# A state space stage whose output stands channels by tokens: paired TensorE products, and decays along tokens read back through DRAM

## The chip, the cores and the metric

The kernel runs on one core of one Trainium2 chip. The metric is the device time of one execution in microseconds (us). The core has a matrix engine (TensorE, PE in the profile; its weight loads are shown apart as PEld), a vector engine (VectorE, DVE), a scalar engine (ScalarE, ACT), GpSimd (POOL) and a sync engine (SyncE, SP), which here issues nearly all direct DMAs. Each engine runs its own instructions strictly in the order in which they stand in its queue; they wait for one another through semaphores. TensorE writes to PSUM, of which the kernel uses eight banks: four as single tiles named `bank`, four as two double tiles named `banks`.

## The reference, cut to what matters

The model is a convolution and attention layer on an image (2 x 256 channels x 48 x 48), a state space (Mamba 2) layer on the 2 x 2304 tokens that it gives, and a routed layer of eight experts. Only the middle one is touched. For a token with normed input `xn` it computes

```
z, x, B, C, dt = split(W_in xn)            # 512, 512, 64, 64, 8 (heads of 64 channels)
x, B, C        = silu(conv over 4 tokens)
dt             = softplus(dt + dt_bias);  a = dt * -exp(A_log)          # per head
state[head]    = exp(a) * state[head] + dt * outer(x[head], B)          # 64 x 64 per head
y[head]        = state[head] C + D[head] * x[head]
out            = W_out( rmsnorm(y * silu(z)) ) + residual
```

The recurrence is computed in chunks of 128 tokens: within a chunk by a masked product of decays and B C, between chunks by a carried state. The square mean of the RMS norm runs over all 512 channels of a token, so that its factor is one number per token and can be applied behind `W_out`.

## The kernel before

**Tiling.** The 4608 tokens are 36 chunks of 128 tokens; three chunks are a block of 384 (`NJ`, `TB`), so there are 12 blocks. `mamba` (L541) is a loop over steps, one chunk a step. In each step it issues the stages of a hand-written pipeline, the oldest chunk first: `out_stage` of the chunk four steps back, `turn_stage` of three back, `y_stage` of two back, `state_stage` and `decay_stage` of the last one and `token_stage` of this one. Every third step also issues the block's front stages: `norms`, `project_0`, `project_1`, `gates_0`, `gates_1` and `sums`. After every six chunks `gate` picks the experts of their tokens (a generator, spread over the stages of the following steps) and scatters the rows to the experts' table `xs`, two indirect DMAs per chunk, issued by GpSimd (L912). The final order of each engine's queue is fixed when the program is built: the instructions of neighbouring stages are mixed there.

**What a step does before the change.** y has tokens on partitions.

- `gates` (L654) multiplies normed tokens (as the stationary operand) with two slices of 264 columns of `W_in`: 256 of z, and 8 of dt or of the router. z is passed through Silu (L665); dt gets its bias (L669); the router's part is made into `gp` (L670). `sums` (L687) makes three short products of the log decays `a`: sums from the chunk's start, sums to its end, and totals; L697 and L699 take their exponentials, `ex` and `et`.
- `project_1` ends with Silu on x (`xc`, L635) and on B and C (`bc`, L636), and moves C to partitions 0 to 63 by a DMA (`ct`, L638).
- `token_stage` (L722): GpSimd spreads `a` over a 128 x 1024 mask, `al` (L730). TensorE transposes B (L734) and x (four times 128 x 128, L737) so that tokens are on partitions; ScalarE copies them out (`btt` L739, `xt` L741). VectorE makes `xd` = x dt (L743), GpSimd `xw` = xd times the decay to the chunk's end (L745), and `y` = x D (L747).
- `decay_stage` (L749): two products of 512 columns sum `al` (L755), ScalarE takes the exponential (`mt`, L764); the product of B and C (L760), masked (`gm`, L762), is multiplied in (L765).
- `state_stage` (L767): one product of 512 columns gives what the chunk adds to the state, on 64 partitions (L773); another of 512 columns with contraction 64 gives what the old state gives to y (L776). VectorE scales the old state (L781), adds (L782), and multiplies the other product by the decay from the chunk's start (`yi`, L784), which with tokens on partitions is one number per partition and head; GpSimd adds it to y (L785).
- `y_stage` (L787): eight products, one per head, with the 128 x 128 `mt` stationary and 64 columns of `xd` moving (L794); VectorE adds y (L795), GpSimd multiplies by z (L796), ScalarE squares and sums along the row (L799), and `rsqrt` (L164: one VectorE and one GpSimd instruction, L169 and L170) gives `rg`, one number per token.
- `turn_stage` (L803) transposes y in four pieces (`transposes`, L518: products at L525, a ScalarE copy at L527). `out_stage` (L811) multiplies with `W_out` (L821, 264 columns, four pieces), adds the residual (L825), and stores the rows to `acc` by a DMA on SP's queue (L832).

The convolution layer ahead of this stage is used in the prediction for comparison: its `score` (L408) multiplies two attention heads on the two halves of the array's rows, one after the other, and `mix` (L469) gives two heads to the two halves of its columns.

Of the kernel before, what the change touches and what calls it, by code (L numbers as in the profile page):

```python
# [55 lines left out]
ZH = DI // 2  # L56

ZG = ZH + SH
XBC = 2 * ZG
# [20 lines left out]
for _name, _k in (  # L80
    ("bq", NH), ("bk", NH), ("bv", NH), ("bp", 1), ("w1", NH * 9), ("w2", NH * 9), ("norm_w", NH),
    ("gnorm_w", DI // P), ("conv_w", NM * 4), ("conv_b", NM),
):
    _VEC[_name] = (_n, _n + _k)
    _n += _k
# [4 lines left out]
for _name, _k in (  # L90
    ("dt_bias", SH), ("A_log", SH), ("Dp", SH), ("bg", E), ("rate1", 1), ("rate2", 1),
):
    _ROW[_name] = (_n, _n + _k)
    _n += _k
# [32 lines left out]
class Kernel:  # L127
# [352 lines left out]
    def mamba_weights(self):  # L480
# [4 lines left out]
        wout = wts.tile([P, DI // P, C + E], F32, name="wout")  # L485
# [7 lines left out]
    def scale_weights(self):  # L493
# [3 lines left out]
        wg = [l1["win"][:, k, ZG + ZH : XBC] for k in range(NH)]  # L497
# [4 lines left out]
        for k in range(NH):  # L502
            for w in (l1["win"][:, k, : ZG + ZH], l1["win"][:, k, XBC:]):
                nc.gpsimd.tensor_scalar(w, w, v["norm_w"][:, k : k + 1], None, ALU.mult)
        turned = self.att.tile([P, NH, P], F32, tag="turned", name="turned", bufs=1)
        for m in range(DI // P):
# [34 lines left out]
    def mamba(self, ctx):  # L541
# [5 lines left out]
        front = (self.norms, self.project_0, self.project_1, self.gates_0, self.gates_1, self.sums)  # L547
        stages = ((self.out_stage, 4), (self.turn_stage, 3), (self.y_stage, 2), (self.state_stage, 1),
# [4 lines left out]
        for step in range(-NJ * 2, nchunk + 4):  # L553
            for p in reversed(range(len(front))):
                k, r = divmod(step + len(front) - 1 - p, NJ)
# [10 lines left out]
            done = step - 3  # L566
# [63 lines left out]
    def project_1(self, k):  # L630
# [3 lines left out]
        xc, bc = block["xc"], block["bc"]  # L634
        nc.scalar.activation(xc, xc, AF.Silu)  # L635
        nc.scalar.activation(bc, bc, AF.Silu)  # L636
        ct = block["ct"] = self.m.tile([DS, TB], F32, tag="ct", name="ct", bufs=3)
        nc.sync.dma_start(ct, bc[DS:P, :])  # L638
# [15 lines left out]
    def gates(self, block, j):  # L654

        nc = self.nc
        xn, win = block["xn"], self.l1["win"]
        cols = slice(3 + j * P, 3 + (j + 1) * P)
        ps = self.banks()
        for h in range(2):  # L660
            self.project(
                ps[:, h, :ZG], lambda k: xn[:, k, cols], lambda k: win[:, k, h * ZG : (h + 1) * ZG]
            )
        z = block["z", j] = self.m.tile([P, DI], F32, tag="z", name="z", bufs=7)
        nc.scalar.activation(z.rearrange("p (h q) -> p h q", h=2), ps[:, :, :ZH], AF.Silu)  # L665
        if j == 0:
            block["dt"] = self.small.tile([P, NJ, SH], F32, tag="dt", name="dt")
            block["gp"] = self.small.tile([P, NJ, E], F32, tag="gp", name="gp")
        nc.vector.tensor_tensor(block["dt"][:, j, :], ps[:, 0, ZH:ZG], self.r["dt_bias"], ALU.add)  # L669
        nc.vector.scalar_tensor_tensor(  # L670
            block["gp"][:, j, :], ps[:, 1, ZH:ZG], block["kap"][:, j : j + 1], block["msw"][:, j, :],
            ALU.mult, ALU.add,
        )

    def gates_0(self, k):
        for j in range(2):
            self.gates(self.blocks[k], j)

    def gates_1(self, k):
        nc, block = self.nc, self.blocks[k]  # L680
        self.gates(block, 2)
        dt = block["dt"]
        self.softplus(dt)
        a = block["a"] = self.small.tile([P, NJ, SH], F32, tag="a", name="a")
        nc.vector.tensor_tensor(a, dt, bcast(self.l1["na"], 1, [P, NJ, SH]), ALU.mult)

    def sums(self, k):  # L687

        nc, small, block = self.nc, self.small, self.blocks[k]
        n = NJ * SH  # L690
        a = block["a"].rearrange("p j s -> p (j s)")
        ps = self.bank()
        nc.tensor.matmul(ps[:, 0:n], lhsT=self.c["le"], rhs=a, start=True, stop=True)
# [499 lines left out]
```

## Time and profile before

| what | value |
|---|---|
| time, median of 3 runs | 1740.0 us (1737.6 to 1740.46) |
| the profiled execution | 1738.11 us, its span 1736.2 us |
| granted TensorE clock, mean | 0.933 of full |
| state space stage, about | 400 to 1065 us of the span |
| a step of it | first `al` products at 441.7 us, last chunk's at 1002.7 |
| instructions | 20936 |

One execution is recorded by the hardware profiler. The page first gives each engine's busy time and share of the span; then the span in 40 equal slices of 43.4 us, each digit the busy share in tenths, and in the row PEclk the clock that the chip granted to TensorE. Further views give groups of instructions (line, engine, operation, output and inputs, shapes, count, busy time and mean ns of one), the waits (who waited for whom: total us, times, longest us), the timeline (start us, length us, engine, line, operation) and the busy time in chosen stretches (for each engine busy us and instruction count). The start of an instruction in TensorE's timeline is sharp; its length reaches into the next one's, since products are pipelined. In float32 each product is recorded twice, and so is its weight load; a transpose is recorded once. "Idle before" is time in which the engine had nothing to run.

### The profile page before, as it was taken

Reading aid. Unit: us, or ns where it says so; the run is one execution under the profiler, and the core shown is the slowest. Engines: PE = TensorE matmul, PEld = TensorE weight load, DVE = VectorE, ACT = ScalarE, POOL = GpSimd, SP = SyncE. Lnnn points to the kernel's source line nnn. Section 1 sums busy time; section 2 is a strip of 40 time slices with the busy share of each in tenths; the row PEclk is TensorE's granted clock in tenths of the full one; section 3 lists DMA queues with packets and bytes.
Section 4 is the critical chain, followed back from the end, with each engine's and each line's share of the span. In section 5 each row is a group of like instructions: output and inputs, shape, how many; then the busy total and the mean of one; then the engine's idle time right before and its main releaser. Section 6 shows DMA issues by size and latency. Waiting matters only on the chain.

```text
span 1736.2 us, 20936 instructions
## 1 busy us (share of the span) xinstructions
PE 1532.9 (88%) x7366; PEld 1134.7 (65%) x7366; DVE 924.3 (53%) x2337; ACT 721.2 (42%) x1564; POOL 562.2 (32%) x505
## 2 busy tenths in 40 slices
PE   2999999987899879798897962999999999999994
PEld 1556565654566556464555542888888888888883
DVE  5867669996787878677786754111111111111111
ACT  0565667885655445453553410222222222222221
POOL 5020000001456565556656763122222222222220
PEclk9898999998998898898898975999999999999997
DMA  6222231111000010101001012666666666666646
GB/s 226 82 72 91 94 112 38 49 37 54 3 10 11 25 34 12 41 13 33 24 12 46 13 47 81 211 194 194 198 192 196 199 200 196 199 198 200 195 137 224
DMA packets 78658, 182.18 MB, mean 105 GB/s; under 512 B 7677, under 2 KB 69526, under 8 KB 72214
## 3 DMA queue, kind: packets, MB, share of 16 engines
q1 hardware_dynamic: 61894, 159.00, 26.3%
q0 software_dynamic: 15840, 21.05, 6.6%
q8 instruction: 59, 0.97, 0.2%
q10 hardware_dynamic: 820, 0.79, 0.1%
q14 instruction: 45, 0.37, 0.1%
HBM read 138.98 MB, written 47.95 MB: 108 GB/s over the span
## 4 chain that ended last, share of the span: by engine, by line
PE 66%; DVE 13%; POOL 8%; ACT 5%; DMA 3%; issue 2%; SPq 1%; DVEq 0%; POOLq 0%; ACTq 0%
PE bank L1023 17%; PE po L1037 17%; PE bank L539 4%; POOL xs L912 3%; PE banks L539 3%; PE bank L469 3%; PE bank L351 2%; PE bank L794 2%; PE bank L374 2%; PE bank L821 2%; PE bank L525 2%; DVE x L312 2%; PE bank L332 2%; PE banks L450 2%; PE banks L408 1%
## 5 line engine op out<-in xcount | busy, mean ns | idle before, releaser
L1027 ACT ACTIVATE hid<-bank,wt 128x256 f32<-128x256 f32 x344 | 163.0, 474 | 442.8 <-PE bank L1023 442.8
L1023 PE MATMUL bank<-ext,wt 128*128 128x256 f32 x1376 | 306.8, 381 | 1.0 <-DVE ext L527 0.8
L1037 PE MATMUL po<-wt,hid 128*128 128x256 f32 x1376 | 304.3, 379 | 0.0
L1043 POOL DMA_INDIRECT acc<-ey,ex x86 | 134.3, 1562 | 494.6 <-DVE ey L1041 334.9
L1023 PEld LDWEIGHTS bank<-ext,wt 128*128 128x128 f32 x1376 | 263.1, 191 | 38.0 <-DVE ext L527 1.2
L1037 PEld LDWEIGHTS po<-wt,hid 128*128 128x128 f32 x1376 | 258.2, 190 | 33.4
L527 DVE COPY ext<-bank 128x512 f32<-128x512 f32 x43 | 29.7, 692 | 281.9 <-PE bank L525 281.9
L1040 DVE TENSOR_TENSOR ey<-po,wt 128x256 f32<-128x256 f32 x86 | 36.5, 424 | 172.0 <-PE po L1037 171.9
L312 DVE SCALAR_TENSOR_TENSOR x<-hid,w2r,x 128x1128 f32<-128x1128 f32 (+3 forms) x72 | 99.2, 1379 | 0.6
L861 POOL TENSOR_SCALAR u<-cst 128x1 int32<-128x1 f32 x36 | 8.6, 246 | 279.0 <-PE bank L469 277.1
L539 PE MATMUL bank<-xn,win 128*128 128x387 f32 x240 | 94.1, 536 | 3.3 <-ACT xn L527 2.9
L426 ACT ACTIVATE prob<-prob,top 128x308 f32<-128x308 f32 x144 | 78.3, 548 | 34.3 <-DVE top L414 34.3
L652 DVE SCALAR_TENSOR_TENSOR xc<-bank,vec,xc 128x384 f32<-128x384 f32 x144 | 81.7, 611 | 20.0 <-ACT xc L648 19.2
L539 PE MATMUL banks<-win,xn 128*128 128x264 f32 x288 | 90.7, 451 | 0.0
L312 DVE SCALAR_TENSOR_TENSOR hid<-xp,vec,hid 128x1128 f32<-128x1128 f32 (+3 forms) x64 | 88.3, 1387 | 0.0
L912 POOL DMA_INDIRECT xs<-u,rows x72 | 75.7, 1052 | 35.3 <-issue 19.1
L755 PE MATMUL banks<-al,cst 128*128 128x512 f32 x144 | 78.2, 643 | 5.2 <-ACT mt L764 4.6
L730 POOL TENSOR_TENSOR al<-cst,a 128x1024 f32<-128x1024 f32 x36 | 68.6, 1913 | 43.7 <-DVE taken L902 14.5
L796 POOL TENSOR_TENSOR y<-y,z 128x512 f32<-128x512 f32 x36 | 47.1, 1307 | 106.7 <-DVE y L795 49.6
L469 PE MATMUL bank<-pt,val 110*64 110x128 f32 (+1 forms) x864 | 76.5, 282 | 4.4 <-ACT pt L453 4.3
L469 PEld LDWEIGHTS bank<-pt,val 110*64 110x64 f32 (+1 forms) x864 | 61.8, 138 | 26.8 <-issue 15.0
L794 PEld LDWEIGHTS bank<-xd,mt 128*128 128x128 f32 x576 | 71.3, 200 | 8.6 <-PE bank L525 3.5
(228 smaller groups left out, 2641.3 us busy)
## 6 DMA issues: line engine op xcount, KB each, us to landing
wt<-in_We SPq DMA_DIRECT2D x43, 2184.0 KB
ex<-xs SPq DMA_DIRECT2D x43, 265.0 KB
val<-vtab SPq DMA_DIRECT2D x72, 110.0 KB
vtab<-vraster SPq DMA_DIRECT2D x18, 396.0 KB
vraster<-vout SPq DMA_DIRECT2D x22, 256.0 KB
x<-in_x SPq DMA_DIRECT2D x4, 1152.0 KB
acc<-x SPq DMA_DIRECT2D x36, 128.0 KB
t<-acc SPq DMA_DIRECT2D x12, 384.0 KB
```

The source lines that it names most:

```text
L312: nc.vector.scalar_tensor_tensor(dst, src, w[:, k : k + 1], dst, ALU.mult, ALU.add)
L426: nc.scalar.activation(prob[:, a, :], prob[:, a, :], AF.Exp, bias=top[:, a : a + 1], scale=-1.0, accum_out=den[:, a : a + 1],)
L469: nc.tensor.matmul(po[j * HD : (j + 1) * HD, :P], lhsT=val[:nk, i, a * HD : (a + 1) * HD], rhs=pt[:nk, j, i, :], start=i == 0, stop=i == l ...
L539: self.nc.tensor.matmul(ps, lhsT=lhs(k), rhs=rhs(k), start=k == 0, stop=k == NH - 1)
L652: nc.vector.scalar_tensor_tensor(out, ps[:, i : i + TB], wc[:, i : i + 1], out, ALU.mult, ALU.add)
L755: nc.tensor.matmul(pd[:, k, :], lhsT=self.c["gt"], rhs=al[:, 4 * k : 4 * k + 4, :].rearrange("p s t -> p (s t)"), start=True, stop=True,)
L794: nc.tensor.matmul(py[:, cols], lhsT=mt[:, s, :], rhs=xd[:, cols], start=True, stop=True)
L912: put = nc.gpsimd.indirect_dma_start(self.xs, bass.IndirectOffsetOnAxis(ap=rows[:, i, k : k + 1], axis=0), u2[:, i, :], None)
L1023: nc.tensor.matmul(ps[:, :TR], lhsT=w1[:, k, c * P : (c + 1) * P], rhs=xt[:, k, :], start=k == 0, stop=k == NH - 1,)
L1027: nc.scalar.activation(hid[:, c, :], ps[:, :TR], AF.Gelu, bias=b1[:, c : c + 1])
L1037: nc.tensor.matmul(po, lhsT=hid[:, c, j * P : (j + 1) * P], rhs=w2[:, c, :], start=c == 0, stop=c == NHC - 1)
L1043: nc.gpsimd.indirect_dma_start(self.acc, bass.IndirectOffsetOnAxis(ap=token, axis=0), y[:, j, :], None, compute_op=ALU.add)
```

## The change

y now stands with channels on partitions (four pieces of 128 channels) and tokens along the row, from the start to `W_out`.

- z is made with the weights stationary, 384 tokens moving, four pieces of 128 channels per block (in `sums`); dt and the router's part come from six products of 16 columns per block (`gates`, one stage instead of two), and their VectorE work is done once per block.
- `y_stage` has `xd` (64 columns per head) stationary and `mt` (128 columns) moving, two heads to the two halves of the partitions.
- The state stands as 128 x 256: four heads on partitions 0 to 63, four on 64 to 127. What the chunk adds is two products of 256 columns; what the old state gives is four of 128 columns, with B and C taken from `ct` and from the upper half of `bc`.
- The decay from the chunk's start must now run along tokens. `sums` makes it for 8 heads x 384 tokens, stores it to DRAM (`decays`), and `token_stage` loads it back spread over partitions, `rd`, by two DMAs per chunk; neither chunk that begins an image needs it.
- x D is done by ScalarE, four instructions of 128 x 128; `xt` goes. ScalarE squares y, VectorE adds the four pieces up (`sm`), and a product with ones (`square_stage`, three steps back) sums over channels. `turn_stage` is gone; `out_stage` stands three steps back, behind `state_stage`.
- Silu on x, B and C and the DMA of `ct` move from `project_1` to the end of `sums`; `sums` comes one step earlier than it did.

```diff
-        front = (self.norms, self.project_0, self.project_1, self.gates_0, self.gates_1, self.sums)
-        stages = ((self.out_stage, 4), (self.turn_stage, 3), (self.y_stage, 2), (self.state_stage, 1),
+        front = (self.norms, self.project_0, self.project_1, self.gates, self.sums)
+        stages = ((self.square_stage, 3), (self.y_stage, 2), (self.state_stage, 1), (self.out_stage, 3),
                   (self.decay_stage, 1), (self.token_stage, 0))
...
-                k, r = divmod(step + len(front) - 1 - p, NJ)
+                k, r = divmod(step + len(front) - p, NJ)
...
     def gates(self, k):
+        ps = self.bank()
+        for j in range(NJ):
+            cols = slice(3 + j * P, 3 + (j + 1) * P)
             self.project(
+                ps[:, j * 2 * SH : (j + 1) * 2 * SH], lambda k: xn[:, k, cols], lambda k: win[:, k, DI:XBC]
+            )
...
     def sums(self, k):
+        for j in range(NJ):
+            nc.tensor.matmul(
+                ps[:SH, j * P : (j + 1) * P], lhsT=a[:, j, :], rhs=self.c["le"], start=True, stop=True
+            )
+        from_start = small.tile([SH, TB], F32, tag="from", name="from_start", bufs=2)
+        nc.scalar.activation(from_start, ps[:SH, :TB], AF.Exp)
+        nc.sync.dma_start(self.decays[k], from_start)
+        z = block["z"] = self.m.tile([P, NZ, TB], F32, tag="z", name="z")
+        for i in range(2):
+            ps = self.banks()
+            for m in range(2):
+                cols = slice((2 * i + m) * P, (2 * i + m + 1) * P)
+                self.project(ps[:, m, :TB], lambda k: win[:, k, cols], lambda k: xn[:, k, 3:])
+            nc.scalar.activation(z[:, 2 * i : 2 * i + 2, :], ps[:, :, :TB], AF.Silu)
+        nc.scalar.activation(bc, bc, AF.Silu)
+        nc.scalar.activation(xc, xc, AF.Silu)
+        nc.sync.dma_start(ct, bc[DS:P, :])
...
     def token_stage(self, c):
-        nc.scalar.copy(xt, px)
-        nc.gpsimd.tensor_tensor(hp(y), hp(xt), bcast(self.r["Dp"], 2, wide), ALU.mult)
+        for m in range(NZ):
+            nc.scalar.mul(y[:, m, :], block["xc"][:, m, cols], self.v["Dp"][:, m : m + 1])
+        if c % (NBLK * NJ):
+            rd = ch["rd"] = self.m.tile([P, NZ, P], F32, tag="rd", name="rd")
+            by_head = self.decays[c // NJ].rearrange("(m i) t -> i m t", i=2)
+            for i in range(2):
+                nc.sync.dma_start(
+                    rd[i * HD : (i + 1) * HD], bcast(by_head[i][:, cols], 0, [HD, NZ, P])
+                )
...
     def state_stage(self, c):
-        nc.tensor.matmul(pst[:DS, :], lhsT=ch.pop("btt"), rhs=ch.pop("xw"), start=True, stop=True)
+        for g in range(2):
+            nc.tensor.matmul(
+                pst[g * DS : (g + 1) * DS, :half], lhsT=btt, rhs=xw[:, g * half : (g + 1) * half],
+                start=True, stop=True,
+            )
-            nc.tensor.matmul(ps, lhsT=block["ct"][:, ch["cols"]], rhs=old, start=True, stop=True)
+            ps = self.banks()
+            for m in range(2):
+                for g in range(2):
+                    rows = slice(g * DS, (g + 1) * DS)
+                    nc.tensor.matmul(
+                        ps[:, g, m * P : (m + 1) * P], lhsT=old[rows, m * P : (m + 1) * P],
+                        rhs=(block["bc"][rows, cols] if g else block["ct"][:, cols]), start=True, stop=True,
+                    )
...
     def y_stage(self, c):
-            nc.tensor.matmul(py[:, cols], lhsT=mt[:, s, :], rhs=xd[:, cols], start=True, stop=True)
+            m, i = divmod(s, 2)
+            nc.tensor.matmul(
+                py[i * HD : (i + 1) * HD, m * P : (m + 1) * P], lhsT=xd[:, s * HD : (s + 1) * HD],
+                rhs=mt[:, s, :], start=True, stop=True,
+            )
-        nc.scalar.activation(sq, y, AF.Square, accum_out=ss)
+        nc.scalar.activation(sq, y, AF.Square)
+        nc.vector.tensor_reduce(sm, sq.rearrange("p m q -> p q m"), AX.X, ALU.add)
+
+    def square_stage(self, c):
+        nc.tensor.matmul(ps[:, 0:1], lhsT=ch.pop("sm"), rhs=self.ones[:, 0:1], start=True, stop=True)
+        self.rsqrt(rg, ps[:, 0:1], 1e-5, 1.0 / DI)
-
-    def turn_stage(self, c):
-        self.transposes(
-            yt.rearrange("p k q -> p (k q)"), [y[:, k * P : (k + 1) * P] for k in range(DI // P)]
-        )
```

More of the change, by code (lines that the diff above doesn't have):

```diff
@@ L669, in gates @@
[L669 to L672, printed above, removed]
-        )
[L675 to L682, printed above, removed]
+        both = ps[:, : NJ * 2 * SH].rearrange("p (j i s) -> p j i s", j=NJ, i=2)
@@ L785, in state_stage @@
+        nc.vector.tensor_tensor(hp(state), hp(old), bcast(over, 2, [P, SH // 2, HD]), ALU.mult)
+        nc.vector.tensor_add(state, pst[:, :half], state)
+        yi = self.m.tile([P, NZ, P], F32, tag="yi", name="yi")
+        nc.vector.tensor_tensor(
+            yi.rearrange("p (g m) q -> p g (m q)", g=2), ps[:, :, :half],
+            ch.pop("rd").rearrange("p (g m) q -> p g (m q)", g=2), ALU.mult,
+        )
         nc.gpsimd.tensor_add(y, y, yi)
```

127 lines of the change are left out of this document (62 added, 65 removed).

## The prediction

> **What bounds the kernel now.** I read first the engine totals and the 40 slices on the page. TensorE is busy for 88% of the span, and the change lies in one stage only: the state space part, slices 10 to 24 (about 400 to 1065 us). The experts after it (PE 9, DVE 1) and the convolution before it stay as they are.
>
> ```profile
> PE 1532.9 (88%) x7366; PEld 1134.7 (65%) x7366; DVE 924.3 (53%) x2337; ACT 721.2 (42%) x1564; POOL 562.2 (32%) x505
> ...
> PE   2999999987899879798897962999999999999994
> ...
> POOL 5020000001456565556656763122222222222220
> PEclk9898999998998898898898975999999999999997
> ```
>
> An average over that stage hides two regimes, so next I asked for busy time by stretches (columns PE, PEld, DVE, ACT, POOL, then the granted clock).
>
> ```profile
> 620.00:683.00 63.00, 59.61 (x281) 40.15 (x279) 51.92 (x127) 36.02 (x62) 35.72 (x29) 1.00 0.05 13
> 683.00:722.00 39.00, 26.68 (x94) 15.21 (x93) 26.56 (x92) 11.07 (x18) 25.05 (x28) 0.83 0.11 39
> 727.00:792.00 65.00, 60.68 (x286) 41.47 (x285) 51.74 (x130) 37.52 (x63) 38.23 (x31) 0.98 0.06 16
> 792.00:831.00 39.00, 28.56 (x97) 16.94 (x97) 26.02 (x93) 11.84 (x21) 25.94 (x27) 0.75 0.12 39
> ```
>
> About 65 of every 106 us (six chunks) are **saturated**: PE 59.61 of 63, VectorE 51.92, at full clock. The other 40 are the **gate stretch**: PE 26.68 of 39, clock 0.83. The view of PE's waits tells what ends last there.
>
> ```profile
> PE bank L737 <- DVE gm L762: 24.5, 4, 7.5
> PE bank L891 <- DVE cnt L888: 9.9, 4, 2.7
> PE bank L773 <- POOL xw L745: 9.4, 6, 1.9
> ```
>
> Four waits of 5 to 7.5 us behind VectorE, which waits for ScalarE's squares, which wait for POOL's `y*z` behind a run of scatters (L912), one each 1.27 us in the timeline. So PE's own work sets the pace in the saturated stretches, and the POOL queue in the gate stretches. The spacings used below are differences of starts in PE's timeline of one saturated step; one step (a chunk of 128 tokens) takes 16 us (35 steps from 441.7 to 1002.7).
>
> ```profile
> 671.45 0.60 PE L525 MATMUL bank<-cst,y 128*128 128x128 f32 x4
> 671.88 0.61 PE L539 MATMUL banks<-win,xn 128*128 128x264 f32 x2
> 672.33 1.02 PE L755 MATMUL banks<-al,cst 128*128 128x512 f32 x2
> 673.19 1.90 PE L794 MATMUL bank<-xd,mt 128*128 128x64 f32 x16
> 675.01 1.07 PE L773 MATMUL bank<-xw,btt 128*64 128x512 f32 x2
> 676.02 1.12 PE L776 MATMUL bank<-state,ct 64*128 64x512 f32 x2
> 676.98 0.38 PE L760 MATMUL bank<-ct,bc 64*128 64x128 f32 x2
> ```
>
> **Do paired products run side by side?** The convolution stage already has both kinds of pair, on halves of the columns (L469) and of the rows (L408).
>
> ```profile
> 253.92 1.81 PE L469 MATMUL bank<-pt,val 110*64 110x128 f32 x24
> 255.66 1.32 PE L408 MATMUL banks<-kp,q 64*128 64x308 f32 x8
> ```
>
> Each product is two records. L408: 1.25 us to the next start for 8 records of 308 columns, 156 ns each or 0.51 ns a column; L755, not paired, takes 0.86 us for 2 records of 512, 0.84 ns a column. L469: 1.74 us / 24 = 72 ns for 128 columns, against 111 for 128 at L755's rate. So both kinds overlap.
>
> **The change, TensorE, a step.** (1) The four transposes of y go: 0.43 us. (2) The eight y products had 64 columns behind a 128-column weight load: 1.82 us, 114 ns a record. They become 128 columns behind 64, in column pairs: 16 records at L469's 72 ns are 1.15, at the 55 ns of perfect pairs 0.88; I take 1.0. Saved 0.8. (3) State in, L773: 1.01 us becomes four records of 256 columns in column pairs, by L408's rate 0.52, plus a little for the short group: 0.55. Saved 0.45. (4) State out, L776: 0.96 becomes eight records of 128 in row pairs, 0.52. Saved 0.45. Sum: -2.1 us a step, -6.4 a block of three. Added to a block: z is 16 records of 384 columns, 323 ns each as L539's 387-column records in the timeline, 5.2 us, for 24 records of 264 at 222 ns, 5.3; dt and router logits become 12 records of 16 columns at the weight-load spacing of 114 ns, +1.4; the sums have three more short products, +0.3; the three square sums about 0.25 each (L693 to L695: 14 us over 36 products recorded twice, less than 0.4), +0.75. Net -6.4 + 2.3 = **-4.1 us a block, -1.4 a step**.
>
> [...]
>
> **VectorE, a step.** Two state operations shrink from 64x512 (962 and 678 ns) to 128x256 (bounds 353, L1041, and 678; I take L1040's 424): -0.8. A reduce of 512 elements to 128 is new and strided: no such row; bounds 0.2 (L908, 48 elements) and 1.33 (L765, 1024 elements); I take 0.68, the mean of the 512-element operations. Gates: 36 x (150 + 212) ns go, 36 of some 200 come: -0.16. Net -0.3 on 51.92/63 x 16 = 13.2, so 12.9 us. But the reduce waits for ScalarE's square (630 ns), that for POOL's `y*z` (1268), that for VectorE's own y addition. In the new order only two state operations stand between in one step of three (0.85 us): a stall of 1.27 + 0.63 - 0.85 = 1.05 us and more, with the residual, gm and mt queued behind it, and PE's next products behind mt. After PE, VectorE is what is late next: 14.6 us of PE against 12.9 and such waits.
>
> **ScalarE** loses xt, yt, the accumulator read and three z (589 + 586 + 188 + 596, x36: -70 us), gains 144 scalings of 128x128 (bounds 201 for 64 elements and 375 for 256; I take 300: +43), 24 z of 768 (between 596 and 1025; +19), the exponentials (+4), and 14 more table loads by the instruction order (86 for 72, 1283 ns: +18): +14 us over 36 steps. It is busy 36 of 63, so the spare time hides it; uncovered it is 14 us. **POOL** loses `x*D`, 36 x 1122 = -40 us. In the saturated stretches it is busy 57%: worth nothing there. In the gate stretches the new order helps (`y*z` now stands ahead of the scatters) and hurts (`xw` and `al` behind ten of them): I count 0.
>
> **DMA and SP.** 68 loads of `rd`, each 256 runs of 512 B, and 12 stores of the decays. Queue 1's 61894 packets took 26.3% of 16 engines' span, 118 ns each: 512 x 118 / 16 = 3.8 us a step, and 2.6 us to landing (the scatter's row; no load's is shown). They are issued a step before use, about 15 us ahead: hidden. On SP they wait for `yi` two chunks back, with ct and the acc stores behind; those have a step as well. ct itself comes two steps later than before: between 0 and 1 us a block of wait, 0 to 12 us; I take 0.
>
> **The sum.** Saturated: 440 to 1000 us less four gate stretches of 40 is 400 us, 25 steps. Of the 1.4 I take 1.0, since VectorE stands only 1.7 below the new PE time and the reduce takes 1 back: -25. One stage less at the drained end (transposes 0.9 us at half clock, copy 0.6, their hops): -2. Gate stretches 0. Together -27. The profiled execution took 1738.1 us (span 1736.2 and 1.9 around it) and would take 1711; it lies 1.9 under the median of 1740.0, so the forecast is **1713 us**.
>
> **Rivals.** *Full gain*: VectorE's waits on PE (27.8 us for y) shrink with PE, and the -1.4 holds in all 36 steps, with -2: -52, 1688. For it: PE 95% busy. Against: the gate stretches wait for POOL. *VectorE and the square chain take over*: the stall and ScalarE's later Silu eat 25 of 27: 1738. For it: 82% VectorE already. *Slower*: in the gate stretch the state-in products wait for `xw`, which the new POOL order puts behind ten scatters: 10 x 1.27 = 12.7 us, less 1 us of y products ahead, 11.7 idle where the four waits are 6.1 on average: +5.6 x 4 = +22. With half the saturated gain (-12) this gives 1750. It decides if PE reaches those products when the scatters begin. Against: where PE is behind it has other work to run first, as it had for 6 us of the scatters from 709.3 on. *It doesn't do what it says*: pairs do not overlap; then only the transposes go (-1.3 a block), the additions (+2.3) stay and the shorter loads give 0.5: +6, 1746. Against: L408 and L469.
>
> One more thing could go either way: PE at less load may be granted less clock. In the timeline y's 16 records take 1.82 us at 673.19 and 3.76 at 681.92 with no wait between; just ahead ten transposes ran. [...]
>
> **Numbers.** Forecast case (1690 to 1730) 0.45, full gain 0.15, VectorE takes over 0.14 (half of it within 0.2%, the rest to either side), slower by the scatters 0.19, no overlap 0.07. Within 0.2% (1736.5 to 1743.5, about what a measurement tells from no change) 0.08; faster 0.66; slower 0.26. Range: from somewhat beyond full gain, 1675, to the slower rival with the ct bound partly on top, 1755.
>
> **What would show it.** Right: y's 16 records near 1.0 us, state in and out near 0.55; PE's busy time in the stage down by some 40 us; VectorE's new waits at the reduce about 1 us; saturated steps of 15 us. Wrong: records of the pairs one after the other; PE waiting at state-in for `xw` more than 8 us in each gate stretch; waits on `rd`; more stretches at half clock.

## The result, and the profile after

The changed kernel takes 1763.2 us (median of 4 runs, 1754.0 to 1765.5) against 1738.8 us for the kernel before in the same job (1737.2 to 1740.5): **ratio 1.013, 95% interval 1.0091 to 1.0169**. It is slower, outside the forecast's range. Its profiled execution took 1754.0 us (span 1752.2), the lowest of the four, so the trace shows less than the median's loss: 16.0 us of span against 24 us.

The totals and slices of the changed kernel's page:

```profile
PE 1516.7 (87%) x7690; PEld 1108.7 (63%) x7690; DVE 907.2 (52%) x2337; ACT 747.4 (43%) x1602; POOL 510.8 (29%) x469
...
PE   3999999987888878788887862899999999999994
...
POOL 5020000002345554645546553122222222222220
PEclk8899999997999889898898886899999999999997
```

TensorE is busy 16 us less and VectorE 17, but in slices 10 to 25 the 9s of PE became 8s, and the mean granted clock fell from 0.933 to 0.925. Most of the loss lies in that stage: from the first to the last addition of y, 580.5 us before and 595.9 after. The first addition itself came 5.7 us later (at 466.9 us, before at 461.2). The way from the last addition to the experts got shorter (40.9 to 38.8), and so did the experts and what follows (653.7 to 650.5).

The products themselves became what the change makes of them. PE's timeline of one clean step of the changed kernel (start, time, out and in, count, then the idle time before):

```profile
663.12 2.77 PE L539 MATMUL bank<-xn,win 128*128 128x387 f32 x8
665.73 0.28 PE L846 MATMUL bank<-ones,sm 128*128 128x1 f32 x2
665.94 1.09 PE L831 MATMUL bank<-mt,xd 128*64 128x128 f32 x16
666.86 0.60 PE L797 MATMUL bank<-xw,btt 128*64 128x256 f32 x4
667.39 1.12 PE L776 MATMUL banks<-al,cst 128*128 128x512 f32 x2
668.36 1.94 PE L860 MATMUL bank<-wout,y 128*128 128x264 f32 x8
```

From start to start, y's 16 records take 0.92 us (before 1.82) and state in 0.53 (1.01). State out, seen where it stands in one piece, is 0.65 (0.96):

```profile
687.22 0.37 PE L806 MATMUL banks<-ct,state 64*128 64x128 f32 x1
687.23 0.37 PE L806 MATMUL banks<-bc,state 64*128 64x128 f32 x1
...
687.87 1.98 PE L776 MATMUL banks<-al,cst 128*128 128x512 f32 x4
```

Pairs overlap; that is not where the time went.

Now the same window of the stage in both kernels (columns PE, PEld, VectorE, ScalarE, POOL, clock). Before:

```profile
440.00:1020.00 580.00, 503.89 (x2120) 327.98 (x2119) 444.23 (x1181) 279.51 (x475) 351.98 (x306) 0.91 0.07 21
```

After:

```profile
440.00:1020.00 580.00, 475.59 (x2383) 297.73 (x2381) 420.64 (x1167) 300.80 (x511) 297.24 (x264) 0.89 0.12 36
```

Every engine but ScalarE is less busy, and yet the work moves on more slowly, so what is added is time in which engines stand. (At 1020 us the changed kernel is also less far on, so the same window holds less of its work; busy times of the whole execution compare equal work.) The waits of that window in the changed kernel (us in total, times, longest), from the views of VectorE, ScalarE and PE:

```profile
DVE rs L169 <- PE bank L846: 43.2, 12, 6.2
DVE sm L840 <- ACT sq L838: 28.1, 14, 6.1
...
ACT sq L838 <- POOL y L836: 133.8, 29, 13.7
...
PE bank L746 <- DVE lg L865: 18.0, 9, 4.7
...
PE bank L797 <- POOL xw L755: 12.4, 4, 3.7
```

and the two in the kernel before that they replace:

```profile
DVE rs L169 <- ACT sq L799: 29.6, 12, 7.8
...
ACT sq L799 <- POOL y L796: 76.6, 22, 7.5
```

VectorE stands still twice in one norm now: at the sum over parts, and again for the square product, which TensorE reaches only in its own order. Together 71.3 us against 29.6. The idle time that the forecast's slower rival named, PE at state in behind `xw`, is there, but 3.7 us at most at the four gates of this window, where the rival needed 11.7; at the end of the stage it is once 9.4 (at 1048.8).

The view that explains most is worked out from the trace: the time from one chunk's first y product to the next one's, over four rounds of six chunks from chunk 5 on (means, us; a gate falls once in six). Half clock is the sum of the clock records below full speed (all of them 0.5) between the first and the last addition of y.

| kernel | s1 | s2 | s3 | s4 | s5 | s6 | sum | half clock, stage |
|---|---|---|---|---|---|---|---|---|
| before | 18.9 | 17.8 | 8.7 | 28.6 | 24.3 | 8.6 | 106.9 | 117.6 |
| changed | 19.9 | 14.6 | 20.2 | 19.5 | 25.0 | 11.0 | 110.1 | 144.8 |
| before, no norm (e3) | 18.8 | 16.2 | 8.8 | 29.2 | 16.5 | 8.6 | 98.1 | 55.0 |
| changed, no norm (e2) | 20.2 | 12.3 | 21.2 | 16.8 | 20.9 | 10.1 | 101.4 | 115.4 |
| before, no scatters (e9) | 18.9 | 17.8 | 8.7 | 28.4 | 15.7 | 8.6 | 98.1 | 61.4 |
| changed, no scatters (e10) | 21.1 | 14.6 | 21.2 | 20.1 | 14.7 | 10.3 | 101.9 | 123.4 |
| before, neither (e11) | 19.5 | 16.2 | 8.8 | 29.2 | 15.3 | 8.5 | 97.5 | 51.2 |
| changed, neither (e12) | 21.4 | 12.3 | 21.6 | 16.8 | 12.4 | 10.1 | 94.6 | 82.2 |

The order of the stages differs, so a step of one kernel does not hold the same work as the same step of the other (PE is busy 8.6 us of s3 before and 17.2 after); sums of neighbouring steps are safer to compare. In s2 17.8 became 14.6 us, with PE busy 17.5 of it before and 12.2 after, but there VectorE is busy 13.1 of the 14.6. With its neighbours s6 and s1, the steps without a gate, nothing is left of that: 45.3 us before, 45.5 after. The steps s3 to s5, in which the gate falls, took 61.6 and take 64.7.

### The profile page after: what moved, and what is told of

It is laid out like the page before. It is cut to its first block, busy times and chain, and to the rows that moved or that the text cites. A ratio compares the mean times of both kernels' runs of the same rounds, so it can differ in the third digit from the quotient of the medians.

```text
span 1752.2 us, 21776 instructions
## 1 busy us (share of the span) xinstructions
PE 1516.7 (87%) x7690; PEld 1108.7 (63%) x7690; DVE 907.2 (52%) x2337; ACT 747.4 (43%) x1602; POOL 510.8 (29%) x469
## 5 line engine op out<-in xcount | busy, mean ns | idle before, releaser
L776 PE MATMUL banks<-al,cst 128*128 128x512 f32 x144 | 91.7, 746 | 8.2 <-DVE yi L818 5.6
L838 ACT ACTIVATE sq<-y 128x512 f32<-128x512 f32 x36 | 22.6, 628 | 154.6 <-POOL y L836 154.6
L539 PE MATMUL banks<-xn,win 128*128 128x384 f32 x192 | 80.7, 552 | 8.5 <-ACT mt L785 8.5
L860 PE MATMUL bank<-wout,y 128*128 128x264 f32 x288 | 85.1, 445 | 0.4 <-DVE y L835 0.4
L647 DVE SCALAR_TENSOR_TENSOR xc<-bank,vec,xc 128x384 f32<-128x384 f32 x144 | 78.1, 610 | 8.6 <-ACT xc L643 8.4
```

Source lines behind the costliest of these rows:

```text
L539: self.nc.tensor.matmul(ps, lhsT=lhs(k), rhs=rhs(k), start=k == 0, stop=k == NH - 1)
L647: nc.vector.scalar_tensor_tensor(out, ps[:, i : i + TB], wc[:, i : i + 1], out, ALU.mult, ALU.add)
L776: nc.tensor.matmul(pd[:, k, :], lhsT=self.c["gt"], rhs=al[:, 4 * k : 4 * k + 4, :].rearrange("p s t -> p (s t)"), start=True, stop=True,)
L860: nc.tensor.matmul(ps[:, : C + E], lhsT=y[:, k, :], rhs=self.l1["wout"][:, k, :], start=k == 0, stop=k == NZ - 1)
```

## The experiments

Four sets. Of each: the edit, what was on record, what came. Ratios are to the kernel before in the same job.

### Where the order stands, and what is loaded

**e1** puts the output stage back to four steps behind, first in the step, as the kernel before has it; **e5** adds a buffer for y, since e1 made ScalarE wait for one.

```diff
-        stages = ((self.square_stage, 3), (self.y_stage, 2), (self.state_stage, 1), (self.out_stage, 3),
+        stages = ((self.out_stage, 4), (self.square_stage, 3), (self.y_stage, 2), (self.state_stage, 1),
...
-            done = step - 2
+            done = step - 3
```

> The changed kernel with out_stage put back to four steps behind the newest chunk, ahead of square_stage, as it stood before; everything else stays. Theory CHAIN (the norm's way through ScalarE, VectorE, TensorE and GpSimd got longer and has one step less to run in, so that VectorE's queue, in order, waits for it): the wait of VectorE before L169 on TensorE's square product (43 us in the changed kernel) and before the reduce (28 us) shrink to under half, and the time falls from 1763 to 1725-1740. Rival LOAD (the decays' way through DRAM): no change, 1760-1766. Rival SILU (Silu on x, B, C too late): no change, 1760-1766. Rival CLOCK (less TensorE work, so less clock): no change or a few us.

> The run with out_stage four steps back, with a sixth buffer for y, since ScalarE was seen there to wait 69 us for a free y (L760 behind the output product). CHAIN in its first form (too few steps for the norm): that wait hid the gain, so now 1730-1750. If the norm's distance is not it: 1755-1765, at most what the y buffer gives.

e1: 1768.9 us, 1.0175 (1.0156 to 1.0194). e5: 1764.1, 1.0158 (1.0135 to 1.018). The missing step of slack is not the cause: giving it back gains nothing. Yet VectorE's wait for the square product, 43.2 us in the changed kernel, is gone from both traces. In e1 (window 440 to 1000) a wait for the output product stands in its place:

```profile
DVE x L864 <- PE bank L860: 49.9, 15, 6.5
```

So that wait only moved.

**e4** takes the loads of the decays away (`rd` is a constant tile of halves, so the part of y from the state is wrong by the decays). **e8** takes the three Silu and the copy of ct back to where they were, in `project_1`.

```diff
-                nc.sync.dma_start(
-                    rd[i * HD : (i + 1) * HD], bcast(by_head[i][:, cols], 0, [HD, NZ, P])
-                )
```

> The changed kernel without the 68 loads of the spread decays: a tile of halves stands in their place, so the decay from the chunk's start is left out of y. LOAD: the time falls by 10 us or more, to 1735-1753. CHAIN, SILU, CLOCK: 1758-1766, since no instruction of the trace was seen waiting for these loads.

> The changed kernel with Silu on x, B and C and the load of ct put back to the end of project_1, as before; five table loads fewer by the instruction order (81 for 86). SILU (they come too late, and TensorE's transposes and the ct load wait for them): 1740-1755. CHAIN and WAITS: 1758-1768.

e4: 1758.0, 1.011 (1.0093 to 1.0127). e8: 1763.7, 1.0162 (1.014 to 1.0184). Some 5 us lie in the loads, not clear of the intervals, and none in the Silu. The decays' way through DRAM is nearly hidden, as forecast.

### The norm, and the products alone

**e2** and **e3** leave the norm out of the changed kernel and of the one before (squares, sum, root; the factor is one).

```diff
-        nc.scalar.activation(sq, y, AF.Square)
-        nc.vector.tensor_reduce(sm, sq.rearrange("p m q -> p q m"), AX.X, ALU.add)
...
-        nc.tensor.matmul(ps[:, 0:1], lhsT=ch.pop("sm"), rhs=self.ones[:, 0:1], start=True, stop=True)
-        self.rsqrt(rg, ps[:, 0:1], 1e-5, 1.0 / DI)
+        ch["rg"] = self.ones[:, 0:1]
```

> The changed kernel without the norm's factor: squares, their sums, the square product and the reciprocal root are left out and the factor is one. CHAIN: the time falls by 30 us or more, to 1700-1730, far more than the 24 us of VectorE work, 8 us of TensorE work and 23 us of ScalarE work it leaves out would give where they are hidden, and more than the same cut gives in the kernel before. LOAD, SILU, CLOCK: it falls by no more than it does in the kernel before (5-12 us), to 1750-1758.

> The kernel before with the same part left out (squares, their row sums, reciprocal root; the factor is one): the measure for the run above. CHAIN: there the factor has a step to arrive, so 1725-1737, a gain of 2 to 13 us, mostly from the 30 us that VectorE waited there for the squares in the gate stretches. All others: the same.

e2: 1704.8, 0.9823 (0.9798 to 0.9848). e3: 1700.3, 0.9796 (0.9761 to 0.9831). The norm costs 58 us in the changed kernel and 38 before, where 2 to 13 had been expected; and without it the change still gains nothing. In e2 the largest wait of PE is the slower rival's:

```profile
PE bank L797 <- POOL xw L755: 34.6, 5, 11.8
```

So with the norm gone the next wait, behind the scatters, takes its place at once. The 11.8 us fall at the end of the stage (at 998.6); in the four gates before, this wait is 4.1 to 7.4 us.

**e6** makes only the state products paired in the kernel before. **e7** issues the kernel before's root a step later, in `turn_stage`, so that VectorE does not stand behind ScalarE's squares.

```diff
-        nc.tensor.matmul(pst[:DS, :], lhsT=ch.pop("btt"), rhs=ch.pop("xw"), start=True, stop=True)
+        for g in range(2):
+            nc.tensor.matmul(
+                pst[g * DS : (g + 1) * DS, :half], lhsT=btt, rhs=xw[:, g * half : (g + 1) * half],
+                start=True, stop=True,
+            )
```

> The kernel before with one part of the change alone: the state as 128 x 256 and its products paired (two of 256 columns for what the chunk adds, two of 256 columns for what the old state gives), tokens still on partitions, no decays through DRAM. It takes 0.9 us a step off TensorE in L773 and L776 (by the changed kernel's 0.53 and 0.65) and 0.6 off VectorE in the two state operations. If pairing pays where nothing else changes (theory CHAIN: the loss lies in what came with it): 1715-1730. If TensorE's time was never worth anything, since the queues wait on each other anyway (theory WAITS): 1733-1742.

> The kernel before with the reciprocal root (L169, L170) issued one step later, at the head of turn_stage, with nothing else changed. It takes away VectorE's wait for ScalarE's squares (29.6 us in 12 waits in the kernel before, behind the scatters). CHAIN: a queue that waits for the norm costs what it waits, so 1710-1730. WAITS: VectorE would wait for something else at the same place, 1733-1742.

e6: 1737.0, 0.9992 (0.998 to 1.0005). e7: 1738.2, 1.0007 (0.9994 to 1.0021). In e6 the same window has

```profile
440.00:1020.00 580.00, 476.85 (x2291) 327.00 (x2290) 424.35 (x1185) 281.16 (x477) 332.21 (x307) 0.90 0.07 21
```

27.0 us less of TensorE (503.89 before) and 19.9 less of VectorE, for no time at all. The steps tell where it went: s1, s2 and s3 get 2.7 us shorter together, s4 and s5 4.2 longer. PE gets to the gate stretch sooner and waits there:

```profile
PE bank L539 <- ACT et L703: 40.0, 4, 10.1
```

four times, up to 10.1 us, once a gate. This is the changed kernel's case in small: a stretch that PE paces gets shorter, and the next one starts earlier and ends no sooner. e7 leaves VectorE's wait for the squares at 23.3 us (window 440 to 1000; 29.6 before), so it tells little of what that wait costs.

### The scatters, with and without the norm

**e9** to **e12** put plain stores on SyncE, to fixed places of the table, in place of GpSimd's 72 scatters (so the experts get other tokens than theirs, and eight stores fill the rest of the table at the start). e9 and e11 are the kernel before with and without the norm, e10 and e12 the changed one.

```diff
-                put = nc.gpsimd.indirect_dma_start(
-                    self.xs, bass.IndirectOffsetOnAxis(ap=rows[:, i, k : k + 1], axis=0), u2[:, i, :], None
-                )
+                n = 2 * (first + i) + k
+                put = nc.sync.dma_start(
+                    self.xs[n % E * PART + n // E * P : n % E * PART + n // E * P + P, :], u2[:, i, :]
+                )
```

> Kernel before with the 72 scatters of GpSimd in the gate replaced by plain stores on SyncE's queue to fixed places of the table (the tokens land in places that are not theirs, so that the experts work on tokens of other experts; eight stores fill the rest of the table at the start). It takes some 52 us of GpSimd time out of the state-space stage and the ten scatters in one run out of the gate stretch; the wait of the scatter for its row numbers no longer holds GpSimd up. SCATTER theory (GpSimd's queue with the run of scatters sets the two long steps of every six, so that what the products save elsewhere is given back there): state-space stage 15 to 35 us shorter, total 1705 to 1725. WAITS theory (the steps are held by many cross waits of which the scatters are one): stage 0 to 12 us shorter, total 1727 to 1740.

> Changed kernel with the same replacement of the scatters by stores on SyncE to fixed places. SCATTER theory: the paired products' gain appears once GpSimd has no run of scatters, so this falls below the kernel before with the same edit by 10 to 30 us: 1690 to 1710. WAITS theory: it stays above the kernel before with the same edit by 10 to 25 us, as the two kernels do as they stand: 1740 to 1760. CLOCK theory (what TensorE saves it idles, and the granted clock falls): the half-clock time stays 25 us above the other kernel's with the same edit, and the total stays above it.

> Kernel before without the norm's squares, sum and root (factor one, as in the earlier run) and with the scatters replaced by stores on SyncE to fixed places: both of the things that hold GpSimd and VectorE up are gone. Earlier run without the norm alone: 1700.3. SCATTER theory: a further 15 to 30 us shorter, 1670 to 1685, TensorE busy over 90% of the stage, since it is the bound then. WAITS theory: 0 to 12 us shorter, 1688 to 1700.

> Changed kernel with both edits, no norm and stores in place of scatters. Earlier run without the norm alone: 1704.8. SCATTER theory: with TensorE as the only bound left, the paired products' gain of about 1 us a step shows: 20 to 35 us below the kernel before with the same two edits, 1640 to 1660. WAITS theory: within 10 us of the kernel before with the same two edits. CLOCK theory: TensorE's busy time at full clock is lower, but half-clock time 20 us or more above the other kernel's gives most of it back, and the difference is under 15 us.

| us, ratio to before (interval) | whole | no norm | no scatters | neither |
|---|---|---|---|---|
| before | 1738.8 | 1700.3, 0.9796 | 1684.7, 0.9696 (0.968 to 0.9712) | 1674.9, 0.9649 (0.9633 to 0.9665) |
| changed | 1763.2 | 1704.8, 0.9823 | 1704.4, 0.9823 (0.9801 to 0.9845) | 1649.9, 0.948 (0.9443 to 0.9517) |
| changed less before | +24.4 | +4.5 | +19.7 | **-25.0** |

The last column is the study's answer. Where neither norm nor scatters are there, the change gains 25.0 us. Where either is there, it gains nothing. That the 25.0 lie so near the forecast's 27 is in part luck: the runs of e12 spread over 14 us, the two profiled executions differ by 17.2, and part of the gain stands where the forecast had put none. By steps, s2 gives 3.9 us and s5, in which the scatters stood, 2.9; s1 and s6 take 3.5 back. The two lines of e10 and e12 (window 440 to 970, same columns as above) show what TensorE does with it. e10:

```profile
440.00:970.00 530.00, 458.76 (x2318) 286.28 (x2316) 404.36 (x1128) 299.97 (x506) 237.43 (x206) 0.90 0.14 38
```

e12:

```profile
440.00:970.00 530.00, 468.31 (x2417) 288.26 (x2415) 401.91 (x1164) 273.48 (x469) 239.76 (x194) 0.92 0.15 43
```

In e12 PE is busier and gets more of the work done in the same window (2417 records to 2318). In s2 PE has 11.9 of 12.3 us there: it sets the pace, as the forecast supposed of every clean step. In e10 the same step takes 14.6, with VectorE at 13.1.

The CLOCK theory has half of its signs: in e10 half-clock time is 62.0 us above e9's and the total stays above. But in e12 it is 31.0 above e11's, and the gain is there all the same, where CLOCK had at most 15 us. The SCATTER theory's 1690 to 1710 holds e10's number, but not its way: e10 is above e9, not 10 to 30 us below. There WAITS has the sign (10 to 25 above) and too high a total. e9 fell further than either theory had it, e11 and e12 as far as SCATTER said.

The scatters by themselves are no difference between the kernels: their edit takes about as much from both (54 and 59 us), nearly all of the steps' part from s5 (24.3 to 15.7, 25.0 to 14.7). What differs is the norm: with the scatters gone it costs 9.8 us before (1684.7 less 1674.9) and 54.5 in the changed kernel. In e9 VectorE's wait for the squares shrank from 29.6 to

```profile
DVE rs L169 <- ACT sq L799: 4.6, 12, 0.7
```

(window 440 to 970), while in e10, with the same edit and window, the changed kernel's wait for the square product stays:

```profile
DVE rs L169 <- PE bank L846: 47.3, 12, 6.4
...
DVE sm L840 <- ACT sq L838: 7.5, 15, 1.5
```

The first was made by the scatters; the second is not.

Leaving the norm out does not only take waits away. With the scatters gone it takes 44.4 us of busy time off VectorE in the changed kernel (911.1 in e10, 866.7 in e12) and 11.0 before (927.7 in e9, 916.7 in e11); the sum over parts alone is 36 times 1.03 us. Whether the norm costs by its waits or by this work, the four runs do not tell.

### Can the gain be had in a whole kernel?

**e13** issues the root in the output stage, **e14** sums the parts on TensorE with four products, **e16** does both and parts the scatters (two every four yields), **e17** adds to e16 the product of y and z on VectorE. **e15** parts the scatters of the kernel before. **e18** is e13's and e14's edits together with stores in place of scatters.

```diff
-        sm = ch["sm"] = self.m.tile([P, P], F32, tag="sm", name="sm")
-        nc.vector.tensor_reduce(sm, sq.rearrange("p m q -> p q m"), AX.X, ALU.add)
...
-        nc.tensor.matmul(ps[:, 0:1], lhsT=ch.pop("sm"), rhs=self.ones[:, 0:1], start=True, stop=True)
+        for m in range(NZ):
+            nc.tensor.matmul(
+                ps[:, 0:1], lhsT=sq[:, m, :], rhs=self.ones[:, 0:1], start=m == 0, stop=m == NZ - 1
+            )
```

> Changed kernel with the root of the norm (VectorE's scaling of the summed squares from the bank, then GpSimd's power) issued in the output stage, ahead of the update of the residual, in place of right behind the square product at the start of the step. VectorE then no longer stands still behind the square product: in the changed kernel that wait is 43.2 us (12 times, up to 6.2 us). ROOT theory (this wait is what the norm costs in the changed kernel): 25 to 45 us faster than the changed kernel, 1718 to 1738. REDUCE theory (the sum over parts on VectorE, waiting for ScalarE's squares, is): within 8 us of it, 1755 to 1768. WAITS theory (another wait takes its place at once): within 8 us too.

> Changed kernel with the sum of squares over the four parts taken on TensorE: four products with the column of ones into one bank in place of VectorE's sum over parts (about 1 us each of 36, and its wait for ScalarE's squares, 28.1 us in 14 waits) and one product. It takes about 36 us of VectorE work away and adds 3 x 36 short products and weight loads, about 0.1 to 0.4 us each, 11 to 40 us of TensorE. REDUCE theory: 15 to 35 us faster than the changed kernel, 1728 to 1748. ROOT theory: within 10 us of it, the wait for the square product stays. WAITS theory: within 10 us.

> Kernel before with the scatters of the gate issued two every four yields in place of two every yield, and kept in program order: their runs become 7, 1, 1, 1, 1, 1 in place of 9 and 3. SCATTER theory (the run of scatters on GpSimd holds the long step up by 8.6 us of every six steps, the amount that went with stores in place of scatters): 10 to 30 us faster than before, 1708 to 1728. If what costs is the wait for the row numbers or the scatters' total time: within 8 us of before.

> Changed kernel with three edits that leave nothing out: sum over parts on TensorE, root in the output stage, and scatters parted (runs of 4, 3, 2, 1, 1, 1 in place of 10 and 2). Theory that norm and scatters hold it up in turn: most of the gain appears, 1690 to 1720, below both kernels. WAITS theory: 1740 to 1760.

> The kernel of e16 with the product of y and z moved from GpSimd (1.27 us each) to VectorE (an estimate of 0.7 us each, from the additions of the same shape), so that y's addition, the gate by z and the squares need no hop through GpSimd's queue, where the squares wait for it 119.5 us of the window in e16. It leaves nothing out. HOP theory (GpSimd's queue is what holds the norm's way and with it the kernel): 15 to 40 us below e16, 1705 to 1730, below both kernels. WAITS theory (the steps are held by the other ways too): within 8 us of e16, 1738 to 1753; if VectorE's added 25 us count, above it.

> Changed kernel with the sum over parts on TensorE, the root in the output stage, and stores on SyncE to fixed places in place of the scatters (tokens land in places that are not theirs). Against 1704.4 with the scatters' edit alone and 1649.9 with the norm left out too. VECTOR theory (VectorE's two waits in the norm are what the norm costs): 1660 to 1680, under the kernel before with the same scatters' edit (1684.7). HOP theory (GpSimd's hops and TensorE's own extra products make the rest): 1685 to 1700.

| run | us | ratio (interval) |
|---|---|---|
| e13 root in the output stage | 1750.8 | 1.0079 (1.0056 to 1.0102) |
| e14 sum on TensorE | 1755.1 | 1.0103 (1.0086 to 1.012) |
| e15 before, scatters parted | 1736.6 | 0.9994 (0.9982 to 1.0006) |
| e16 both, scatters parted | 1745.7 | 1.0043 (1.0026 to 1.006) |
| e17 and y with z on VectorE | 1734.8 | 0.9989 (0.9974 to 1.0004) |
| e18 both, stores for scatters | 1710.1 | 0.9847 (0.9828 to 0.9866) |

e13 and e14 take 12 and 8 us off the changed kernel's median, with intervals that overlap its own; e16 (17.5 off) stands clear. ROOT and REDUCE had promised 25 to 45 and 15 to 35. Neither run settles its theory: in e13 the wait for the square product is still 38.2 us of 43.2, and in e14 the sum costs on TensorE a good part of what it frees. The changed kernel's row in the window 440 to 1020, and e14's:

```profile
L846 PE MATMUL bank<-ones,sm 128*128 128x1 f32 x64 | 10.0, 225 | 1.0 <-DVE sm L840 0.9
```

```profile
L846 PE MATMUL bank<-ones,sq 128*128 128x1 f32 x256 | 32.4, 248 | 1.0 <-ACT btt L751 0.9
```

22.4 us of TensorE for about 34 us of VectorE. And VectorE's busy time in the whole execution fell by 9.4 us only (907.2 to 897.8), because another of its instructions got longer: the scaling of the state, `state` (L815), took 41.6 us in all for 24.6. It needs 0.42 us where it runs freely; each of its longer runs, up to 5.4 us in e14, ended 0.28 to 0.29 us after a GpSimd addition or multiplication of 128 x 512 had ended. The profile counts that as busy, so this wait is in none of the views of waits. e18 is no faster than e10 (1710.1 to 1704.4) and above both ranges given for it: the VECTOR theory's 1660 to 1680 has fallen, and HOP's 1685 to 1700 was too low.

e15 makes the runs of scatters 7, 1, 1, 1, 1, 1 for 9 and 3 and moves nothing: s5 falls from 24.3 to 20.8 and s1 rises from 18.9 to 21.2. The cost moved along with the scatters.

e17 gives 11 us below e16: GpSimd's hop in the norm's way counts (in e16 ScalarE's squares wait 131.4 us for it in the window 440 to 1020), though less than the 15 to 40 expected. VectorE's busy time fell by 10.1 us (888.5 to 878.4) although it took on 24.6 us of products of y and z: none of the 34 scalings of the state runs long any more (14.0 us in all). What takes the hop's place are a wait for VectorE and one for TensorE's output product:

```profile
ACT sq L838 <- DVE y L836: 67.6, 23, 7.3
ACT y L760 <- PE bank L863: 59.3, 22, 7.7
```

e17 is the best kernel here that leaves nothing out and has all the pairs: level with the kernel before within what was measured, not faster.

## Why the prediction was wrong, point by point

- **Pairs overlap**: right. 0.92, 0.53 and 0.65 us where it took 1.0, 0.55 and 0.52. Y's 0.92 us is 0.04 above the 0.88 of perfect pairs (0.86 by L755's own rate, which gives 108 ns for 128 columns and not 111). State out is 0.13 above its term. Before, both state products took longer than L755's two records of as many columns (state in 1.01, state out 0.96, L755 0.86 us); no run tells whether the 0.13 is of the same kind.
- **TensorE's sum, -1.4 a step, "busy time in the stage down by some 40 us"**: 16.2 us in the whole execution, where the work is equal (1532.9 to 1516.7). Part of the rest is the clock: half-clock time in the stage rose by 27.2 us. State in before took 1.01 us at 675.01 and 1.89 at 685.68, just inside a stretch of half clock (from 685.1 on), so this is up to 13.6 us (an estimate: half of 27.2).
- **y's records of 3.76 us "with no wait between"**: misread. The trace has them busy for 1.90 us, as at full clock; then PE stood 1.85 us waiting for `xw`:

```profile
681.92 1.90 PE L794 MATMUL bank<-xd,mt 128*128 128x64 f32 x16
685.68 1.97 PE L773 MATMUL bank<-xw,btt 128*64 128x512 f32 x2 [1.85 <-POOL xw L745]
```

So the 1.94 us between the two times are no fall of the clock, and the ten transposes ahead tell nothing of one: the stretch of half clock there runs from 685.1 to 695.3 and begins within that wait. With four transposes fewer a step the stretches of half clock became more, 28 for 14.
- **VectorE, 12.9 a step, and a stall of 1.05 us at the sum in one step of three**: the busy time was about right (17.1 us less in the whole execution, some 11 forecast), though the sum took 1027 ns, not 680, and the two state operations 723 and 414 ns, not 424 each. The stalls were mis-sized: 1.05 in one step of three is some 12 us over the stage, and the sum alone waited 28.1. The second stop, the root behind the square product, was not in the working at all: 43.2 us.
- **ScalarE, +14, hidden**: +26.2 in the whole execution; e8 shows that its later Silu are hidden. **POOL, -40**: -51.4, worth nothing by itself, as said. **DMA, 0**: e4 gives some 5 us.
- **"Saturated: ... 25 steps. Of the 1.4 I take 1.0"**: the step that failed first. Clean steps were taken to be TensorE's and to get 1.0 us shorter each; s6, s1 and s2 together take 45.5 us for 45.3. s2 is 3.2 us shorter, but there VectorE is the pace then (13.1 of 14.6 us; without norm and scatters 10.2 of 12.3, with PE 11.9).
- **"Gate stretches 0"**: the step that failed beside it. s3 to s5 cost 3.1 us more a round, and the round of six 3.2. PE comes to them earlier and then stands behind other engines' queues; e6 shows the same in the kernel before with nothing but paired state products.
- **The end, -2**: right (40.9 to 38.8).
- **Rivals.** *VectorE and the square chain take over* names half of the cause, and its 1738 was too low since it counted no loss elsewhere. *Slower by the scatters* was right in its sign and not in its way: the wait at state in is 3.7 us at most at the gates of the changed kernel. That wait is the next in line: 4.1 to 7.4 us at the gates of e2, and 11.8 once at the end. *No overlap* is out.
- **The sign named for "wrong", more stretches at half clock**: it came, 28 for 14 in the stage.

What is shown: the change has a gain to give (-25.0 us with norm and scatters away), and the norm and the scatters each suffice to take it. What stays open: how the norm's 54.5 us without scatters divide between VectorE's work for it, VectorE's stops, GpSimd's hop and the clock. Of the stops, the one behind the square product went away in e1 and e5, and another took its place, without gain. Single edits gave 8 to 12 us, the edits of e17 together 28. The clock was not held in any run, so whether its fall is a cause of the lost time or only follows the waits was not tried.

## What to carry to other kernels

Before counting what an engine saves, ask of each step which other engine's queue it next has to wait for, and count both sides of a wait: the instruction that waits, and what stands behind it in the same queue. A stretch that one engine paces gives its gain on only if the stretch after it doesn't start with a wait on something else; do one part of the change alone (as in e6) to see that. And where two causes each suffice, taking either away shows nothing of the gain: take away both. Last, compare the shortest and the mean time of an instruction (0.41 and 0.72 us for the scaling of the state in the changed kernel): a wait inside it counts as busy.

## What the runs showed of the hardware

- The granted clock was not the same from kernel to kernel: half-clock time in the stage was 117.6 us before, 61.4 with the scatters gone, 51.2 with the norm gone too, and in the changed kernel 144.8, 123.4 and 82.2. From the first to the last addition of y the trace has 14 stretches of half clock before and 28 after, each a multiple of 3.4 us long. In the changed kernel idle times of PE of 2.14, 2.45 and 2.45 us (from 542.2, 689.9 and 908.1 on) were followed by 3.4 us of half clock from 546.0, 692.8 and 911.2 on; two others of 2.14 and 2.13 us (from 654.2 and 872.4 on) were not. What makes the clock fall, no run here shows.
- A product with one moving column is not nearly free: 22.4 us for some 96 further products in e14 are 0.23 us each, two records of 0.12. That is what the kernel before paid for a record of 64 columns behind the same 128-column weight load (0.114), where y's paired records, 128 columns behind 64, are 0.058 apart (0.92 us / 16).
- VectorE's sum over four parts at a stride (512 to 128 elements) took 1027 ns, where the additions of 512 elements took 689.
- VectorE's scaling of the state by a decay (128 x 256, both operands in SBUF) took 0.41 to 0.43 us in 21 of 34 runs of the changed kernel. The other 13 took 0.75 to 1.56 us, and each ended 0.28 to 0.29 us after one of GpSimd's multiplications (L836 or L755) had ended. In e17, where the one of y by z is not on GpSimd, all 34 took 0.39 to 0.43.
- Twelve scatters on GpSimd, 1.05 us busy each before and 1.02 after, cost 8.6 us of every six steps before and 10.3 after (s5), and parting them only moved that.
